# A convolution and attention kernel: first pixels ahead of the Toeplitz build, last sums ahead of last stores, two loads on another queue

## The chip, the cores and the metric

The kernel runs on one core of a Trainium2 chip. The metric is the device time of one execution, in microseconds, given as the median of several runs. A profile is one execution in which every instruction of every engine was recorded. The engines are TensorE (PE, with its weight loads as PEld), VectorE (DVE), ScalarE (ACT), GpSimd (POOL) and SyncE (SP). SP, ACT and POOL each also issue DMAs from a queue of their own, in order, mixed with their other instructions.

## The reference

Input x has 64 images of 55 x 55 pixels and 96 channels. Two layers follow each other; cut to what matters:

```python
# layer 0: depthwise 25x25 convolution of which only every third tap is kept
lat = conv(x, raw_kernel * mask)          # 9 x 9 taps, 3 pixels apart, the middle one left out
t = lat * x + bias + x                    # = (lat + 1) * x + bias
# layer 1: each image is a sequence of 3025 tokens
h = relu(bn1(layernorm(t) @ w1.T))        # 192 wide
X = fft(h, axis=tokens); ... diagonal complex map, relu ...; y = ifft(...).real
t = t + bn2(y @ w2.T)
t = t + ffn(layernorm(t))                 # 96 -> 384 -> 96, values rounded to fp8 and fp16
```

The change touches layer 0 and the place where layer 1 takes its sequences over.

## The kernel before

**Toeplitz build.** Taps that lie 3 pixels apart split the image into 3 residue classes of rows (r) and of columns. For each channel the 9 x 9 taps become a block matrix, so that the convolution of some rows is a few matrix products. PE makes these matrices from the taps (kt) and a 0/1 selector (sel, four loads): 56 slabs pt of 4 or 5 columns, each 8 or 10 matmuls into one of 8 PSUM banks (L205). ACT copies channels 0 to 47 of a slab into toep (L214), then DVE copies channels 48 to 95 into later (L215). later is written out to DRAM as tb in six stores on SP (L217), and toep is loaded anew from tb halfway through the convolution. Then the pools of this stage are closed with first.close(), and the buffers of the sums take their room: the first sum in such a buffer waits until everything that used the closed pools is done, the stores of tb among it.

**Convolution.** Work is cut into 12 groups (half of the channels, residue r, half of the images bh). A group has 4 tiles of rows for r = 0 and 3 tiles for r = 1 and 2, and 6 steps of 8 channels. A step loads its tiles' pixels x on SP (L234, 384 KB a tile, two buffers each, two steps ahead; the first two steps are asked for just before the loop). compute() multiplies: per tile and 4 channels, 16 matmuls for an outer tile and 24 for an inner one, into one PSUM bank pl (L253). DVE forms (pl + 1) * x in a buffer buf of the tile (L261, 0.84 us), and POOL adds the bias (L271). A tile has one buf through the six steps, and there are six bufs (NOB).

**Stores.** When a group ends, its bufs go to the DRAM tensor t1 in token order. stores() lists the DMAs of a tile: one large one a row on ACT (288 KB), and three small ones for three rows on POOL; in the last group every second large one is on SP. Most wait in pending and are issued a few at a time during the next group (L326). If the two groups together need more than six bufs, the first tiles' stores are issued at once, right after their last sums (early, L315). In the last group early is 3, so each tile's stores stand ahead of the next tile's sums.

**The order** in the convolution is written out by hand: each queue holds its instructions as the loop issues them. DMAs of SP and ACT take one of eight semaphores in turn, and each waits until that semaphore's last DMA has landed; POOL's DMAs have eight of their own.

**Sequences.** Layer 1 runs as 64 sequences whose tasks are ordered ahead of time by a planner (ordered(), with a cost and a due time for each task). sequence() begins with load(), two DMAs on SP of 112 and 9 rows (L527), into one of five t buffers. DVE takes the statistics (L538), ACT and DVE a root and its inverse (L499, L503), POOL scales (L552), PE turns and multiplies (L565, L586, L601), and so on. Two tables, m1 and m2, are loaded on ACT as the sequences begin, after the last stores on that queue (L67).

Of the kernel before, what the change touches and what calls it, by code (L numbers as in the profile page):

```python
# [11 lines left out]
F32 = mybir.dt.float32  # L12
# [8 lines left out]
B, R, CH = 64, 55, 96  # L21
NTOK = R * R
# [19 lines left out]
NOB = 6  # L42
SU = 21

NR1, NJ = 25, 121
# [3 lines left out]


@with_exitstack
def conv_attn_hybrid(ctx, tc, a, out, t1, tb, gds, eds):
    nc = tc.nc

    def split(n):
# [18 lines left out]
    with ExitStack() as cx:  # L76
        ccst = cx.enter_context(tc.tile_pool(name="c_cst", bufs=1))
        toep = ccst.tile([128, CHH, NE * TQ], F32, tag="toep", name="toep")
        cbias = ccst.tile([128, CH], F32, tag="cbias", name="cbias")
        ps = cx.enter_context(tc.tile_pool(name="c_ps", bufs=8, space=PSUM))  # L80
        xp = cx.enter_context(tc.tile_pool(name="c_x", bufs=2))
# [1 line left out]
        selp = first.enter_context(tc.tile_pool(name="c_sel", bufs=1))  # L83
        pp = first.enter_context(tc.tile_pool(name="prep", bufs=1))
        lp = first.enter_context(tc.tile_pool(name="c_later", bufs=1))
        later = lp.tile([128, CHH, NE * TQ], F32, tag="later", name="later")
        kt = selp.tile([128, CH], F32, tag="kt", name="kt")
        nc.sync.dma_start(kt, a["taps"])
        sel = selp.tile([128, TQ, SU * TQ], F32, tag="sel", name="sel")
# [9 lines left out]
        for n, of in enumerate(vecs):  # L99
            n0, n1 = 4 * CH * n, min(4 * CH * (n + 1), 4 * (H + CH) + 2 * CH)  # L100
# [30 lines left out]
        nc.vector.memset(ones, 1.0 / CH)  # L131
        zero = pp.tile([3 * NR1, CH], F32, tag="zero", name="zero")
        nc.vector.memset(zero, 0.0)
        for of in (toep, later):
            nc.gpsimd.memset(of[:, :, : 2 * TQ], 0.0)
            nc.gpsimd.memset(of[:, :, 16 * TQ :], 0.0)
        make_identity(nc, ident)
# [19 lines left out]
        for k, width in ((1, H), (2, CH)):  # L157
            bn = bns[k]
            v, r, q = (pp.tile([128, width], F32, tag=f"{x}{k}", name=f"{x}{k}") for x in ("v", "sc", "sq"))
# [9 lines left out]
            row, of = (w1e[96:97, :], slice(96, 97)) if k == 1 else (bias2, slice(0, NR1))  # L169
# [28 lines left out]
        for j0 in range(0, TQ, 5):  # L198
            nj = min(5, TQ - j0)
            for e in range(2, 16):  # L200
                pt = ps.tile([128, 512], F32, tag="ps", name=f"pt_{e}_{j0}")
                for jj in range(nj):
                    for p in range(2):
                        u0 = (15 - e + 3 * p) * TQ
                        nc.tensor.matmul(  # L205
                            pt[64 * p : 64 * p + 64, jj * CH : (jj + 1) * CH],
                            sel[:, j0 + jj, u0 : u0 + 64],
                            kt,
                            start=True,
                            stop=True,  # L210
                        )
                src = pt[:, : nj * CH].rearrange("p (n c) -> p c n", n=nj)
                cols = slice(e * TQ + j0, e * TQ + j0 + nj)
                nc.scalar.copy(toep[:, :, cols], src[:, :CHH])  # L214
                nc.vector.tensor_copy(later[:, :, cols], src[:, CHH:])  # L215
        for c0 in range(0, CHH, CC):
            nc.sync.dma_start(tb[:, c0 : c0 + CC], later[:, c0 : c0 + CC])  # L217
        first.close()

        ob = cx.enter_context(tc.tile_pool(name="c_ob", bufs=NOB))
        groups = [(0, r, bh) for r, bh in ((0, 0), (1, 0), (0, 1), (1, 1), (2, 0), (2, 1))]
        halfway = groups[-1]
        groups += [(1, r, bh) for bh in range(BH) for r in range(NR)]
        steps = [(n, c0) for n in range(len(groups)) for c0 in range(0, CHH, CC)]
        xts, bufs_ = {}, {}

        def load(n, c0):
            half, r, bh = groups[n]  # L230
            c1 = half * CHH + c0
            for m in range(NTS[r]):
                x = xp.tile([128, CC, NBS], F32, tag=f"x{m}", name=f"x{m}_{n}_{c0}")
                nc.sync.dma_start(x, a["xc"][bh, sum(NTS[:r]) + m][:, c1 : c1 + CC, :])  # L234
                xts[n, c0, m] = x

        def compute(n, c0, m):
            half, r, bh = groups[n]
# [36 lines left out]
        def stores(n, m):  # L275

            half, r, bh = groups[n]
            rows_, buf, b0 = TPS[r], bufs_.pop((n, m)), bh * BB
            last = n == len(groups) - 1
            nr = len([i for i in range(rows_) if 3 * (rows_ * m + i) + r < R])  # L280
            large, small_ = [], []
            for i in range(nr):
                n0 = (3 * (rows_ * m + i) + r) * R
                large.append((
                    nc.sync if last and i % 2 else nc.scalar,
                    t1[b0 : b0 + BB, half, n0 : n0 + 48, :].rearrange("b (q s) c -> q b (s c)", s=3),
                    buf[at_row(i) : at_row(i) + 16].rearrange("q (b s) c -> q b (s c)", s=3),
                ))


            to = t1[b0 : b0 + BB, half].rearrange("b (y z) c -> y b (z c)", z=R)
# [12 lines left out]
        for step in steps[:2]:  # L304
            load(*step)
        for k, (n, c0) in enumerate(steps):
            nt = NTS[groups[n][1]]
            nxt = NTS[groups[n + 1][1]] if n + 1 < len(groups) else NOB
            ending = c0 + CC == CHH
            early = nt + nxt - NOB if ending else 0  # L310
            for m in range(nt):
                compute(n, c0, m)
                if m < early:
                    for queue, to, of in stores(n, m):
                        queue.dma_start(to, of)  # L315
# [202 lines left out]
    def sequence(b):  # L518
# [3 lines left out]

        def load():
            tt = make(t, "t", [NJ, 2, NR1, CHH])
            tv = t1[b].rearrange("h (j r) c -> j h r c", r=NR1)
            for p0, p1 in split(NJ):
                nc.sync.dma_start(tt[p0:p1], tv[p0:p1])  # L527

# [16 lines left out]
        for i in range(7):  # L545
# [281 lines left out]
        for q in range(5):  # L827
# [23 lines left out]
            k = task("PE", 0.82, at, inverse_k2, [fetched], new=[(py, "psn")], use=[e2])  # L851
            k = task("DVE", 0.65, at, residual, [k], use=[py, t])
# [6 lines left out]
        for i in range(7):  # L859
            g0, ng = 4 * i, min(4, NR1 - 4 * i)  # L860
            xc, xq, pq = ("xc", b, i), ("xq", b, i), ("pq", b, i)
# [31 lines left out]
            k = task("POOL", 0.03 + 0.19 * ng, at - 0.08, centre, [rstd], new=[(xc, "xc")], use=[t, mean])  # L893
            k = task("POOL", 0.03 + 0.18 * ng, at - 0.08, quantise, [k], new=[(xq, "xq")], use=[xc, ("rstdc", b)])
            k = kt = task("PE", 0.054 * ng, at, turn, [k] + ([kt] if i else []), new=[(pq, "psn")] + ([(tq, "tq")] if i == 0 else []), use=[xq])
            turned_.append(task("ACT", 0.1 + 0.087 * ng, at, turned, [k], use=[pq, tq]))
        hq_done = {}
        for s, k in np.ndindex(3, 3):
            n0, n1 = UPT * s, (UPT * (s + 1) if s < 2 else NJ * NR1)
            n = n1 - n0  # L900
# [35 lines left out]
            x = task("PE", 0.45, at, up, turned_[: (3, 5, 7)[s]], new=[(pu, "psw"), (y16, "y16")], use=[tq])  # L936
            x = task("DVE", 1.23, at, cast, [x], use=[pu, y16])
# [177 lines left out]
```

## Time and profile before

| | us |
|---|---|
| median of three runs | 4841.59 (4833.22 to 4843.41) |
| the profiled execution: time | 4838.86 |
| its span, first to last instruction | 4836.9 |
| PE busy | 4443.6 (92%) |
| DVE, ACT, POOL busy | 3228.9, 3015.1, 3055.8 |
| first matmul of the build, of the convolution, of the sequences | 15.83, 86.10, 1016.73 |
| last matmul of the convolution ends | 944.5 |

How to read it: busy times are sums over the whole span, and hide stages with different limits. The page also divides the span into 40 equal slices of 121 us, each digit the busy share in tenths. The chain of waits follows the work that ended last backwards, from each piece to what released it. A timeline row names an engine, a line, an operation, what it writes and reads, how many, and in brackets how long the engine sat idle before it and what ended that. An entry such as "SPq" is a queue issuing DMAs, not moving data.

### The profile page before, as it was taken

The numbers are of one execution on the slowest core, as the hardware profiler recorded it, in microseconds if no ns is written. First come the engines' busy times: TensorE is split into PE (matmuls) and PEld (weight loads), VectorE is DVE, ScalarE is ACT, GpSimd is POOL, SyncE is SP. The second block draws the span as 40 slices with busy tenths as digits, with TensorE's granted clock in tenths as the row PEclk, the third lists the DMA queues.
The fourth block names the chain that finished last, engine by engine and source line by source line (L and its number), as shares of the span: only waits on it lengthen the run. The fifth ranks groups of instructions, "written<-read, shape, count | busy, mean of one in ns | idle before, by whom it ended". The sixth has DMA issues, their size and how long they took to land.

```text
span 4836.9 us, 194306 instructions
## 1 busy us (share of the span) xinstructions
PE 4443.6 (92%) x83314; PEld 3541.4 (73%) x83314; DVE 3228.9 (67%) x7232; ACT 3015.1 (62%) x5947; POOL 3055.8 (63%) x4209
## 2 busy tenths in 40 slices
PE   7998898759999999999999999999999999999996
PEld 6998898747777777777777777777777777777774
DVE  4444353425777777777777777777777777777766
ACT  1000000047888787777887788888778778877774
POOL 1666575725666666666666666666666666666664
PEclk8999999979999999999999999999999999999996
DMA  4688887876666666666666666666666666666652
GB/s 162 166 197 226 223 203 193 192 173 150 170 171 168 165 173 167 162 169 163 166 171 170 166 173 172 168 167 170 169 167 162 168 164 166 168 169 173 169 150 65
DMA packets 572794, 823.10 MB, mean 170 GB/s; under 512 B 62127, under 2 KB 470276, under 8 KB 570268
## 3 DMA queue, kind: packets, MB, share of 16 engines
q1 hardware_dynamic: 442704, 736.10, 56.0%
q10 hardware_dynamic: 113036, 64.71, 7.0%
q0 software_dynamic: 16192, 9.86, 1.1%
q8 instruction: 654, 10.72, 0.9%
q14 instruction: 208, 1.70, 0.1%
HBM read 419.45 MB, written 390.64 MB: 167 GB/s over the span
## 4 chain that ended last, share of the span: by engine, by line
PE 43%; DVE 16%; POOL 12%; DMA 10%; ACT 10%; issue 7%; ACTq 2%; SPq 0%; POOLq 0%; DVEq 0%
PE pl L253 13%; PE pd L741 6%; PE ph L586 4%; PE pf L601 4%; DVE y L916 4%; POOL ot L971 4%; DMA gd<-g 3%; PE px L667 3%; DVE stc L848 3%; PE pd L751 3%; ACT hq L931 3%; DVE m L693 3%; DMA x<-in_xc_dram 2%; PE pq L884 2%; DVE t L842 2%
## 5 line engine op out<-in xcount | busy, mean ns | idle before, releaser
L693 DVE SCALAR_TENSOR_TENSOR m<-px,par,m 128x400 f32<-128x400 f32 x768 | 478.7, 623 | 703.7 <-ACT m L684 416.3
L253 PE MATMUL pl<-x,toep 128*64 128x96 f32 (+1 forms) x18432 | 791.7, 250 | 91.0 <-DVE buf L261 39.3
L253 PEld LDWEIGHTS pl<-x,toep 128*64 128x64 f32 (+1 forms) x18432 | 786.3, 137 | 96.4 <-issue 46.8
L916 DVE CAST y<-pu 128x1008 f16<-128x1008 f32 (+1 forms) x576 | 690.3, 1198 | 182.0 <-PE pu L907 182.0
L261 DVE SCALAR_TENSOR_TENSOR buf<-pl,x 121x384 f32<-121x384 f32 (+1 forms) x480 | 390.5, 843 | 492.3 <-PE pl L253 310.8
L931 ACT ACTIVATE hq<-z 128x1008 fp8e5<-128x1008 f16 (+1 forms) x576 | 606.2, 1052 | 135.6 <-DVE z L919 130.2
L586 PE MATMUL ph<-w1e,tnt 97*121 97x192 f32 x3200 | 674.6, 335 | 3.0 <-ACT e L780 0.8
L601 PE MATMUL pf<-h,f 121*128 121x384 f32 (+1 forms) x1664 | 667.1, 501 | 2.1 <-ACT h L595 1.9
L271 POOL TENSOR_TENSOR buf<-buf,cbias 121x768 f32<-121x768 f32 (+1 forms) x240 | 433.6, 1820 | 355.8 <-DVE buf L261 336.3
L586 PEld LDWEIGHTS ph<-w1e,tnt 97*121 97x121 f32 x3200 | 531.6, 185 | 141.7 <-DVE t L842 15.9
L499 ACT ACTIVATE sm_s_a<-sm_v_a,eps 121x25 f32<-121x25 f32 x64 | 20.3, 317 | 950.1 <-POOL sm_v_a L490 950.1
L595 ACT ACTIVATE h<-ph 121x384 f32<-121x384 f32 (+1 forms) x832 | 402.7, 485 | 177.8 <-PE ph L586 177.5
L667 PEld LDWEIGHTS px<-m,gt 50*64 50x64 f32 x24576 | 398.6, 135 | 126.3 <-issue 81.0
L667 PE MATMUL px<-m,gt 50*64 50x50 f32 x24576 | 447.8, 221 | 16.8 <-issue 7.7
L971 POOL TENSOR_TENSOR ot<-t,o 121x480 f32<-121x480 f32 x320 | 361.1, 1128 | 117.1 <-DVE o L965 117.1
L741 PEld LDWEIGHTS pd<-w2e,sm 128*64 128x64 f32 x8192 | 351.8, 138 | 113.5 <-issue 58.6
L605 ACT COPY g<-pf 128x384 f32<-128x384 f32 (+1 forms) x832 | 393.5, 473 | 61.7 <-PE pf L601 45.8
L700 POOL TENSOR_TENSOR sr<-ar,m 128x400 f32<-128x400 f32 x128 | 132.7, 1036 | 444.1 <-DVE m L693 434.1
L741 PE MATMUL pd<-w2e,sm 128*64 128x96 f32 x8192 | 410.0, 251 | 0.4 <-ACT h L595 0.4
L565 PE MATMUL pa<-ident,xa 121*96 121x121 f32 x1600 | 241.5, 268 | 162.3 <-POOL xa L552 72.2
L552 POOL TENSOR_TENSOR xa<-t,rstda 121x384 f32<-121x384 f32 (+1 forms) x448 | 346.9, 780 | 60.4 <-PE pa L565 55.4
L951 PEld LDWEIGHTS <-hq 128*121 128x121 fp8e5 x4800 | 331.5, 142 | 54.5 <-issue 21.7
(115 smaller groups left out, 8597.2 us busy)
## 6 DMA issues: line engine op xcount, KB each, us to landing
gd<-g SPq DMA_DIRECT2D x768, 192.0 KB
gt<-gd SPq DMA_DIRECT2D x512, 288.0 KB
x<-in_xc_dram SPq DMA_DIRECT2D x240, 384.0 KB
t<-t SPq DMA_DIRECT2D x64, 1050.0 KB
out_dram<-ot SPq DMA_DIRECT2D x320, 210.0 KB
t<-buf ACTq DMA_DIRECT2D x211, 288.0 KB
ed<-e SPq DMA_DIRECT2D x384, 150.0 KB
ed<-e SPq DMA_DIRECT2D x128, 131.2 KB
```

The lines of the kernel that those rows point to most:

```text
L253: nc.tensor.matmul(pl[p : p + width, cc * NBS : (cc + 1) * NBS], toep[:, c0 + g + cc, o : o + width], xts[n, c0, m + d][:, g + cc, :], sta ...
L271: nc.gpsimd.tensor_tensor(part, part, cbias[:px, c1 : c1 + CC].unsqueeze(1).to_broadcast([px, NBS, CC]), ALU.add)
L586: nc.tensor.matmul(x[:NJ, q * H : (q + 1) * H], live[tnt][:, g * NJ : (g + 1) * NJ], w1e, start=True, stop=True,)
L595: nc.scalar.activation(live[h][:, : nq * H], live[ph][:NJ, : nq * H], AF.Relu)
L601: nc.tensor.matmul(x[:, : nq * H], f1, live[h][:, : nq * H], start=True, stop=True)
L605: nc.scalar.copy(live[g][:, q0 : q0 + nq].rearrange("p q c -> p (q c)"), live[pf][:, : nq * H])
L667: nc.tensor.matmul(x[to : to + 64].rearrange("p (q r n) -> p q r n", q=2, r=2)[:, k2p, :, o : o + NR1], y[rows, k % KC, c0 : c0 + 64], m1[ ...
L693: nc.vector.scalar_tensor_tensor(live[out_], view(px)[:, :, 256 : 256 + KC * NR1], scale, live[than], ALU.mult, ALU.max)
L741: nc.tensor.matmul(y[k % 2][64 * k2p : 64 * k2p + 64, k // 2 * CH : (k // 2 + 1) * CH], full[:, k, 64 * k2p : 64 * k2p + 64], w2e[:, 0, :] ...
L916: nc.vector.tensor_copy(live[y16][:, :n], live[pu][:, :n])
L931: nc.scalar.activation(live[hq][:, k, n0 : n0 + n], live[z16][:, :n], AF.Copy, saturate=False)
L971: nc.gpsimd.tensor_tensor(halves(y), live[t][:, :, 5 * q : 5 * q + 5], halves(live[o16]), ALU.add)
```

## The change

Six things are changed. The first two steps' pixels are asked for at the very top, ahead of taps and selectors. The group list, which now stands there too, begins with r = 1 for each half of the images where it began with r = 0. later is three tiles of 16 channels; each slab's copy by DVE is three copies, and each of the six stores reads one of the tiles. In the last group no tile's stores are issued inside the loop over tiles; all come after the last sum. t1 is two tensors, one for each half of the images. Sequences 0 and 1 are loaded by one DMA each on GpSimd's queue; the other 62 as before.

```diff
-        later = lp.tile([128, CHH, NE * TQ], F32, tag="later", name="later")
+        later = [lp.tile([128, CPL, NE * TQ], F32, tag=f"later{k}", name=f"later{k}") for k in range(CHH // CPL)]
+        groups = [(0, r, bh) for r, bh in ((1, 0), (0, 0), (1, 1), (0, 1), (2, 0), (2, 1))]
+        halfway = groups[-1]
+        groups += [(1, r, bh) for bh in range(BH) for r in range(NR)]
+        steps = [(n, c0) for n in range(len(groups)) for c0 in range(0, CHH, CC)]
...
+        for step in steps[:2]:
+            load(*step)
         kt = selp.tile([128, CH], F32, tag="kt", name="kt")
         nc.sync.dma_start(kt, a["taps"])
...
-        for of in (toep, later):
+        for of in (toep, *later):
             nc.gpsimd.memset(of[:, :, : 2 * TQ], 0.0)
             nc.gpsimd.memset(of[:, :, 16 * TQ :], 0.0)
...
                 nc.scalar.copy(toep[:, :, cols], src[:, :CHH])
-                nc.vector.tensor_copy(later[:, :, cols], src[:, CHH:])
+                for k, of in enumerate(later):
+                    c1 = CHH + CPL * k
+                    nc.vector.tensor_copy(of[:, :, cols], src[:, c1 : c1 + CPL])
         for c0 in range(0, CHH, CC):
-            nc.sync.dma_start(tb[:, c0 : c0 + CC], later[:, c0 : c0 + CC])
+            k, c1 = c0 // CPL, c0 % CPL
+            nc.sync.dma_start(tb[:, c0 : c0 + CC], later[k][:, c1 : c1 + CC])
         first.close()
...
-        groups = [(0, r, bh) for r, bh in ((0, 0), (1, 0), (0, 1), (1, 1), (2, 0), (2, 1))]
...
-        for step in steps[:2]:
-            load(*step)
...
-                if m < early:
+                if m < early and n + 1 < len(groups):
                     for queue, to, of in stores(n, m):
                         queue.dma_start(to, of)
...
-                pending = [x for m in range(max(0, early), nt) for x in stores(n, m)]
+                pending = [x for m in range(nt) if (n, m) in bufs_ for x in stores(n, m)]
...
-            tv = t1[b].rearrange("h (j r) c -> j h r c", r=NR1)
+            tv = t1s[b // BB][b % BB].rearrange("h (j r) c -> j h r c", r=NR1)
+            if b < 2:
+
+                nc.gpsimd.dma_start(tt, tv)
+                return
             for p0, p1 in split(NJ):
                 nc.sync.dma_start(tt[p0:p1], tv[p0:p1])
...
-            t1 = dp.tile([B, 2, NTOK, CHH], F32, tag="t1", name="t1")
+            t1s = [dp.tile([BB, 2, NTOK, CHH], F32, tag=f"t1_{k}", name=f"t1_{k}") for k in range(BH)]
```

More of the change, by code (lines that the diff above doesn't have):

```diff
@@ L42 @@
 NOB = 6
+CPL = 16
 SU = 21
@@ L53, in conv_attn_hybrid @@
 @with_exitstack
-def conv_attn_hybrid(ctx, tc, a, out, t1, tb, gds, eds):
+def conv_attn_hybrid(ctx, tc, a, out, t1s, tb, gds, eds):
     nc = tc.nc
@@ L85, in conv_attn_hybrid, with load @@
         lp = first.enter_context(tc.tile_pool(name="c_later", bufs=1))
-        later = lp.tile([128, CHH, NE * TQ], F32, tag="later", name="later")
+        later = [lp.tile([128, CPL, NE * TQ], F32, tag=f"later{k}", name=f"later{k}") for k in range(CHH // CPL)]
[3 more added lines that the diff above has]
+        steps = [(n, c0) for n in range(len(groups)) for c0 in range(0, CHH, CC)]
+        xts, bufs_ = {}, {}
+        def load(n, c0):
+            half, r, bh = groups[n]
+            c1 = half * CHH + c0
+            for m in range(NTS[r]):
+                x = xp.tile([128, CC, NBS], F32, tag=f"x{m}", name=f"x{m}_{n}_{c0}")
+                nc.sync.dma_start(x, a["xc"][bh, sum(NTS[:r]) + m][:, c1 : c1 + CC, :])
+                xts[n, c0, m] = x
+        for step in steps[:2]:
+            load(*step)
         kt = selp.tile([128, CH], F32, tag="kt", name="kt")
@@ L214, in conv_attn_hybrid @@
                 nc.scalar.copy(toep[:, :, cols], src[:, :CHH])
-                nc.vector.tensor_copy(later[:, :, cols], src[:, CHH:])
+                for k, of in enumerate(later):
+                    c1 = CHH + CPL * k
+                    nc.vector.tensor_copy(of[:, :, cols], src[:, c1 : c1 + CPL])
         for c0 in range(0, CHH, CC):
-            nc.sync.dma_start(tb[:, c0 : c0 + CC], later[:, c0 : c0 + CC])
+            k, c1 = c0 // CPL, c0 % CPL
+            nc.sync.dma_start(tb[:, c0 : c0 + CC], later[k][:, c1 : c1 + CC])
         first.close()
         ob = cx.enter_context(tc.tile_pool(name="c_ob", bufs=NOB))
-        groups = [(0, r, bh) for r, bh in ((0, 0), (1, 0), (0, 1), (1, 1), (2, 0), (2, 1))]
[L224 to L235, printed above, removed]
         def compute(n, c0, m):
@@ L277, in stores @@
             half, r, bh = groups[n]
-            rows_, buf, b0 = TPS[r], bufs_.pop((n, m)), bh * BB
+            rows_, buf = TPS[r], bufs_.pop((n, m))
             last = n == len(groups) - 1
@@ L285, in stores @@
                     nc.sync if last and i % 2 else nc.scalar,
-                    t1[b0 : b0 + BB, half, n0 : n0 + 48, :].rearrange("b (q s) c -> q b (s c)", s=3),
+                    t1s[bh][:, half, n0 : n0 + 48, :].rearrange("b (q s) c -> q b (s c)", s=3),
                     buf[at_row(i) : at_row(i) + 16].rearrange("q (b s) c -> q b (s c)", s=3),
                 ))
-            to = t1[b0 : b0 + BB, half].rearrange("b (y z) c -> y b (z c)", z=R)
+            to = t1s[bh][:, half].rearrange("b (y z) c -> y b (z c)", z=R)
             for i0, (q, ns) in itertools.product(range(0, nr, 3), ((16, 3), (17, 3), (18, 1))):
@@ L1111 @@
             eds = [dp.tile([NR1, 4, KHP, CH], F32, tag=f"e{k}", name=f"ed{k}") for k in range(2)]
-            conv_attn_hybrid(tc, a, out, t1, tb, gds, eds)
+            conv_attn_hybrid(tc, a, out, t1s, tb, gds, eds)
     r = run(nc, [arrays], core_ids=[0])
```

## The prediction

> **What bounds the kernel now.** I read the page's busy slices first, then three stretches: the start, the convolution, and the hand-over to the sequences. The slices show TensorE (PE) nearly full except at two dents, slice 8 and, less deep, the first slices:
>
> ```profile
> PE   7998898759999999999999999999999999999996
> ...
> DMA  4688887876666666666666666666666666666652
> ```
>
> From slice 9 on PE is at 9 tenths to the last slice, and the diff adds or removes nothing there, so those 3,800 us only shift. The change lives in the first 1,020 us. The windows view (columns: stretch, its length, busy time and count of PE, PE loads, VectorE = DVE, ScalarE = ACT, GpSimd = POOL, granted clock, DMA share, GB/s) and the chain of waits for the start:
>
> ```profile
> 40.00:60.00 20.00, 20.00 (x491) 20.00 (x489) 10.42 (x27) 9.87 (x27) 0.00 (x0) 1.00 0.01 4
> 60.00:80.00 20.00, 1.81 (x44) 1.62 (x40) 1.45 (x4) 1.28 (x4) 0.00 (x0) 0.60 0.84 350
> ...
> 100.00:120.00 20.00, 20.00 (x491) 20.00 (x489) 10.83 (x13) 0.00 (x0) 11.57 (x7) 1.00 0.45 140
> ```
>
> ```profile
> 15.83 46.01 PE pt L205 x1064
> ...
> 69.63 17.45 DMA x<-in_xc_dram
> 87.08 0.14 issue
> 87.22 82.94 PE pl L253 x1954
> ```
>
> PE builds the Toeplitz tiles to 61.8, then sits idle for 25 us until 87.2, because the first pixels stand on SyncE's queue (SP) behind the six stores of the second half; meanwhile during the build the DMA engines moved 4 GB/s. A finer windows view dates those stores: 438 GB/s up to 82, a dip in the next line, where the pixels take over, so they are in by about 83.5.
>
> ```profile
> 80.00:82.00 2.00, 0.00 (x0) 0.00 (x0) 0.00 (x0) 0.00 (x0) 0.00 (x0) 0.50 1.04 438
> 82.00:84.00 2.00, 0.00 (x0) 0.00 (x0) 0.00 (x0) 0.00 (x0) 0.00 (x0) 0.50 1.01 263
> ```
>
> The convolution (87 to 944.5) has 18,432 matmul records. One PE timeline row has 734 of them in 30.44 us, 41.5 ns each, so 764 us at full clock; 93 us of the stage is loss. The PE timeline's gaps sum to some 66 us, mostly DVE waiting for a buffer whose store had not landed; the worst is the first line here. The rest is the halved clock after gaps. The hand-over is the second line:
>
> ```profile
> 462.92 5.12 PE L253 MATMUL pl<-x,toep 128*64 128x96 f32 x72 [11.15 <-DVE buf L261]
> ```
>
> ```profile
> 1016.73 1.85 PE L565 MATMUL pa<-ident,xa 121*96 121x121 f32 x8 [72.21 <-POOL xa L552]
> ```
>
> ```profile
> 944.07 1.81 POOL L271 TENSOR_TENSOR buf<-buf,cbias 121x768 f32<-121x768 f32 x1
> ...
> 956.20 1.80 POOL L271 TENSOR_TENSOR buf<-buf,cbias 121x768 f32<-121x768 f32 x1
> 958.30 3.95 POOL L315 DMA_DIRECT2D t<-buf  x6 [0.31 <-POOL buf L271]
> ```
>
> ```profile
> 985.37 23.89 SPq L527 DMA_DIRECT2D t<-t  x10
> ```
>
> ```profile
> 1012.62 1.69 DVE L538 BATCH_NORM_STATS2 sta<-t 121x6 f32<-121x96 f32 x10 [2.82 <-DMA t<-t]
> 1014.23 0.29 DVE L503 RECIPROCAL rstda<-sm_s_a 121x25 f32<-121x25 f32 x1
> 1014.44 2.42 DVE L538 BATCH_NORM_STATS2 sta<-t 121x6 f32<-121x96 f32 x15
> 1017.98 2.49 DVE L538 BATCH_NORM_STATS2 sta<-t 121x6 f32<-121x96 f32 x15 [1.12 <-DMA t<-t]
> ```
>
> The last sum waits until 956.2 behind small stores on POOL, the ten loads start at 985.4 behind SP's nine last stores, and DVE's order makes sequence 0's root wait for sequence 1's load (1012.6) and sequence 1's for sequence 2's (1018.0).
>
> **What the Trainium skill says.** "DMA: Bandwidth & Descriptors", section "Queues, rings and completion order": each DMA engine takes turns between the queues packet by packet. The page of before agrees that packets differ: ACT's queue moved 64.71 MB in 113,036 packets, 572 bytes each, while a row of a sequence's load is 4,800 bytes, so a load beside the stores gets more than its turn. The same page, "Why a DMA increments its semaphore by 16 and not by 1": the number of engines is the largest divisor up to 16 of the slow dimension, 11 for 121 rows, with an exception for GpSimd's queue that uses all; no run shows which. "TensorE: Matmul & The Clock Gate", Part 1: an idle window halves the clock until PE is busy again. The trace agrees: half clock from about 64 to 91.5, so 2 us are lost after 87.2.
>
> **The change part by part.** Queue orders are those of the built program.
>
> *Pixels first.* Six x loads (384 KB each) go ahead of the taps and the four selector loads on SP, so past those, eight pads of ed and the six stores. DMAs of SP and ACT share eight semaphores in turn and each waits for its semaphore's last user, so the first selector load now waits for fw1's landing, fw1's issue for the second x, and taps for the fourth x. 2.36 MB at the 425 GB/s of the 60 to 80 stretch is 5.5 us. But PE's first build matmul was held by pm (14.88), behind ACT's table load at 8.76, not by the selectors; I estimate both at about 16.5 to 17.5. Cost 1.7 us, between 0.5 and, were all queueing exposed, 5.5.
>
> *Three tiles.* 56 copies by DVE become 168. Back to back the old ones start 0.31 us apart (20.57, 20.88, 21.20) for 240 elements; a third each is between 0.10 and 0.31, and I take 0.15, so 0.45 per slab of 0.82 us of PE (46.01/56). Hidden by PE; at 0.31 a slab takes 0.93 and costs 6 us. The last slab adds 0.1. Six memsets in place of two move the same elements on idle POOL. The split doesn't free anything early: in the new program DVE's first sum still waits for all six stores.
>
> *Start of the convolution.* PE may start at about 64 with x there, and fills eight PSUM banks: with the three-tile group first that is 2(16+24+16)+2x16 = 144 matmuls of two records, 144 x 83 ns = 11.9 us. Then it waits for DVE, which waits for the stores: 83.5 + 1.8 = 85.3, one sum of 0.84, so 86.2. Lead against 87.2: 11.9 + 1.0 = **12.9 us**; the half clock is met in both. The next x loads are issued as DVE frees tiles (from 87 on), with 6.6 us of matmuls in hand; covered. Bounds 8 and 14.
>
> *Group order.* With three tiles first, stores begin after 55 us of matmuls instead of 79, and with the lead about 38 us earlier, into a stretch where DMA is at 0.34 to 0.45. Nt runs 3,4,3,4,3,3 instead of 4,3,4,3,3,3, so only two lean groups follow each other before the reload of toep. About 50 of the 93 us of loss lie there (446 to 557). Bounds: nothing, and 25; a loss of 16 if a boundary turns worse (below). I take **8 us**.
>
> *Last sums, two loads on GpSimd.* The three last sums end near 947 instead of 958; 12 small stores move behind them. 18 small stores follow, 0.66 us to issue each, eight semaphores, some 10 us to land: about 22 us, then five memsets (1.3 us), then the loads of sequences 0 and 1 at about 970. They no longer wait behind SP (985.4). SP loses four issues (2.33, 3.01, 1.08, 1.12). Beside the stores they should land near 980 and 988; queued behind them on POOL are only sums that need them. Next late is sequence 2's load on SP, which shares the engines with m1 and m2 (1.87 MB, ACT). DMA was at 0.75 to 0.82 from 944 to 972: moving 2.3 MB there uses about 5 us that were idle, the displaced stores end later by the rest; m1 and m2 no longer take turns with the first loads (3 to 4 us), and the earlier last stores give a few. Sequence 2 in at about 1006 instead of 1018: **12 us**. Bounds 4 (t0 and t1 on few engines, landing after it) and 20.
>
> Sum: 12.9 + 8 + 12 = 33. Profiled execution 4838.9 (span 4836.9 and 2 around it) less 33 is **4806**; the median of 4841.6 is 2.7 above that execution, so 0.7% below.
>
> **Rivals.** (B) One gain is hidden: DMA bounds the convolution (0.8 and more after 180), so its end doesn't move though its start does, or the last stores drain no earlier and sequence 2 lands as before. 0.8 shares that never reach 1 speak for it; PE at 99% in 300 to 400 against. 13 to 20 us left: 4822. (C) The stalls of 446 to 557 vanish and the tail gives 20: 12.9 + 22 + 20, 4784; for it the 40 us of stores moved into idle time, against it the reload that stays. (N) Both of B, with only the head's lead partly kept: 4835. (S) Slower: the place is the boundary between groups. Two neighbouring groups with seven tiles share six buffers, so one tile's stores must land within some 16 us; among the first five boundaries the new order has four such in place of three, and DVE waits there. Price 11.15 plus 5 of half clock, 16 each. It decides from the third stall on, when it eats the 33: with a loss of 16, 4855. Against it: the added boundary comes when no other stores are queued.
>
> **How the numbers follow.** Forecast 0.46 (own range 4796 to 4819), B 0.24, C 0.14, N 0.09, S 0.07. About 0.2% (9.7 us) can be told from no change. B, C and the forecast are faster: 0.84; N same: 0.09; S slower: 0.07. The range reaches to 4781 for C and 4829 for B.
>
> **What would show it.** PE's first pl near 64, a gap from 76 to 86, then full. First ACT stores near 125 instead of 160.8. The end of matmuls near 924. POOL's last sums in a row, its t loads about 25 us after them, PE's pa some 60 us after the last pl instead of 72. Wrong if PE's first pl waits for x, if pt begins after 20, if gaps with DVE buf grow, or if the pace after the hand-over changes from about 60 us a sequence ((4836.9 - 1016.7)/64).

## The result, and the profile after

| | before | after |
|---|---|---|
| median of 20 runs each, us | 4839.79 (4827.8 to 4853.4) | 4816.01 (4798.85 to 4834.27) |
| profiled execution: time; span | 4838.86; 4836.9 | 4798.85; 4797.1 |
| build by PE ends | 61.8 | 60.5 |
| convolution: first matmul; last one ends | 86.1; 944.5 | 60.3; 918.7 |
| first matmul of the sequences | 1016.7 | 971.8 |
| from the convolution's last matmul to the end of the span | 3892.4 | 3878.3 |

The ratio of the times is 0.9948, with a 95% interval of 0.9936 to 0.996: 25 us less, between 19 and 31. The profiled execution of after is the shortest of its 20, so the two profiles stand 40 us apart where the medians stand 24; below, dates from single profiles are used for order and for waits, and amounts are means over several profiles or come from the ratios.

The busy slices of after (tenths in 40 slices of 120 us) answer to the first view of before:

```profile
PE   8999898689999999999999999999999999999996
...
DMA  4788888875666666666666666666666666666662
```

The first three digits of PE were 7, 9 and 9 and are 8, 9 and 9. The dent at the hand-over, a 5 in the ninth digit of before (slice 8, counted from 0), is a 6 in the eighth: it comes earlier. From the tenth digit on the row of nines is the same, only shorter. At the start, PE's timeline of after has (start, length, engine, line, operation, count; in brackets the idle time before and what ended it):

```profile
59.80 0.66 PE L225 MATMUL pt<-kt,sel 128*64 128x96 f32 x12
60.30 11.39 PE L261 MATMUL pl<-x,toep 128*64 128x96 f32 x272
72.52 0.88 PE L261 MATMUL pl<-x,toep 128*64 128x96 f32 x16 [0.83 <-issue]
85.62 14.58 PE L261 MATMUL pl<-x,toep 128*64 128x96 f32 x306 [12.22 <-DVE buf L269]
```

The first pl follows the last pt without a gap, so the pixels were there. PE does 272 + 16 records, which are 144 matmuls of two records each, and then stands for 12.2 us. DVE's timeline and the chain of waits (start, length, what) of after name the cause:

```profile
84.76 5.51 DVE L269 SCALAR_TENSOR_TENSOR buf<-pl,x 121x384 f32<-121x384 f32 x8 [23.39 <-DMA tb<-later]
```

```profile
66.78 17.57 DMA tb<-later
84.76 0.81 DVE buf L269
```

DVE may not write the first sum before the six stores of tb have landed. The idle time has moved from before the first matmul to after the 144th; what was won is the work done ahead of it. The windows view (columns as in the prediction) shows the stores of t coming forward:

```profile
60.00:80.00 20.00, 12.56 (x300) 12.18 (x296) 1.02 (x7) 0.55 (x2) 0.00 (x0) 0.89 0.92 379
120.00:140.00 20.00, 19.97 (x484) 19.86 (x482) 10.24 (x13) 0.00 (x0) 16.31 (x13) 1.00 0.76 186
```

From 120 to 140 DMA is at 0.76 where it was at 0.34; ACT's first store is issued at 127.35 where it was 160.76. At the other end, the timelines of PE, POOL, SP's queue and DVE in after, in this order:

```profile
971.81 1.85 PE L575 MATMUL pa<-ident,xa 121*96 121x121 f32 x8 [53.07 <-POOL xa L562]
```

```profile
915.01 1.81 POOL L279 TENSOR_TENSOR buf<-buf,cbias 121x768 f32<-121x768 f32 x1 [1.08 <-DVE buf L269]
...
919.66 1.78 POOL L279 TENSOR_TENSOR buf<-buf,cbias 121x768 f32<-121x768 f32 x1 [2.83 <-DVE buf L269]
921.38 5.26 POOL L335 DMA_DIRECT2D t<-buf  x8
...
943.53 1.60 POOL L534 DMA_DIRECT2D t<-t  x2
```

```profile
962.77 11.83 SPq L537 DMA_DIRECT2D t<-t  x6
```

```profile
961.62 4.09 DVE L548 BATCH_NORM_STATS2 sta<-t 121x6 f32<-121x96 f32 x25 [42.05 <-DMA t<-t]
966.50 1.70 DVE L548 BATCH_NORM_STATS2 sta<-t 121x6 f32<-121x96 f32 x10 [0.79 <-DMA t<-t]
969.29 0.32 DVE L509 RECIPROCAL rstda<-sm_s_a 121x25 f32<-121x25 f32 x1 [1.09 <-ACT sm_s_a L505]
...
980.08 2.49 DVE L548 BATCH_NORM_STATS2 sta<-t 121x6 f32<-121x96 f32 x15 [8.13 <-DMA t<-t]
982.49 0.30 DVE L509 RECIPROCAL rstda<-sm_s_a 121x25 f32<-121x25 f32 x1
```

POOL's last sum follows DVE's last sum at once, the small stores come after it, and the two loads are issued at 943.5, 19 us before SP issues the next. PE starts on the sequences 53 us after its last matmul of the convolution, where it was 72. But sequence 1's root (982.49) stands on DVE behind statistics of sequence 2, whose load on SP lands only at 980. What that load waits for is in the view of SP's waits from 913 to 980 (engine, line, what for; us in total, times, longest):

```profile
SPq L537 <- DMA t<-buf: 20.6, 3, 10.8
```

Before the first of the load's two DMAs (issued at 962.77) SP waits 10.8 us for a store of its own to land, and before the second, the one of 9 rows (972.67), another 9.6 us for a store of ACT, with which it shares one of the eight semaphores.

### The profile page after: what moved, and what is told of

Read it like the earlier page. It is cut to its first block, busy times and chain, and to the rows that moved or that the text cites. A ratio compares the mean times of both kernels' runs of the same rounds, so it can differ in the third digit from the quotient of the medians.

```text
span 4797.1 us, 194464 instructions
## 1 busy us (share of the span) xinstructions
PE 4431.4 (92%) x83314; PEld 3528.9 (74%) x83314; DVE 3233.7 (67%) x7344; ACT 3011.1 (63%) x5947; POOL 3057.1 (64%) x4215
## 4 chain that ended last, share of the span: by engine, by line
PE 39%; DVE 20%; POOL 13%; DMA 10%; ACT 8%; issue 8%; ACTq 1%; SPq 0%; POOLq 0%; DVEq 0%
PE pl L261 12%; PE pd L751 5%; DVE y L926 4%; DVE stc L858 4%; PE pf L611 4%; PE ph L596 4%; POOL ot L981 4%; DMA gd<-g 3%; PE pd L761 3%; DVE m L703 3%; ACT hq L941 3%; DVE t L852 3%; PE px L677 2%; DMA gt<-gd 2%; DMA t<-buf 2%
## 5 line engine op out<-in xcount | busy, mean ns | idle before, releaser
L261 PE MATMUL pl<-x,toep 128*64 128x96 f32 (+1 forms) x18432 | 784.9, 249 | 73.6 <-DVE buf L269 43.4
L694 ACT ACTIVATE m<-px,par 128x400 f32<-128x400 f32 x384 | 262.6, 684 | 170.8 <-PE px L677 166.3
```

The lines of the kernel that those rows point to most:

```text
L261: nc.tensor.matmul(pl[p : p + width, cc * NBS : (cc + 1) * NBS], toep[:, c0 + g + cc, o : o + width], xts[n, c0, m + d][:, g + cc, :], sta ...
```

## The experiments

None of the twelve leaves out a part of the computation. "Last matmul" is the end of the convolution's last matmul; "2nd root" (the reciprocal of sequence 1 on DVE) and "end" are counted from it. All four dates are from one profiled execution each. "mid" is the sum of PE's gaps over 0.3 us between 430 and 580, around the reload of toep. Each ratio is to runs of before that were taken beside that kernel's, so it isn't the ratio of two medians of this document.

| run | median, us (runs) | ratio, 95% | last matmul | mid | 2nd root | end |
|---|---|---|---|---|---|---|
| before | | | 944.5 | 33.2 | 77.6 | 3892.4 |
| after | 4816.0 (20) | 0.9948 (0.9936, 0.996) | 918.7 | 26.4 | 63.8 | 3878.3 |
| e1_head_only | 4818.4 (9) | 0.9953 (0.9934, 0.9972) | 916.2 | 23.6 | 76.0 | 3886.5 |
| e2_tail_only | 4830.0 (14) | 0.9991 (0.9977, 1.0006) | 946.8 | 31.3 | 63.4 | 3890.2 |
| e3_old_group_order | 4813.0 (8) | 0.9945 (0.9926, 0.9965) | 936.8 | 30.9 | 63.0 | 3880.6 |
| e4_one_later_tile | 4812.6 (12) | 0.9949 (0.9934, 0.9964) | 930.5 | 26.5 | 67.4 | 3880.3 |
| e5_loads_on_sync | 4819.7 (14) | 0.9954 (0.9942, 0.9966) | 937.5 | 24.5 | 68.9 | 3889.1 |
| e6_stores_between_sums | 4819.2 (5) | 0.9961 (0.9948, 0.9974) | 919.5 | 23.6 | 74.2 | 3897.8 |
| e7_three_on_gpsimd | 4810.9 (6) | 0.9938 (0.9915, 0.9962) | 926.2 | 21.4 | 69.0 | 3891.1 |
| e8_five_on_gpsimd | 4812.3 (6) | 0.995 (0.9935, 0.9965) | 928.1 | 24.4 | 68.9 | 3879.0 |
| e9_order_only | 4835.9 (14) | 0.9995 (0.998, 1.0009) | 929.2 | 22.8 | 75.5 | 3893.0 |
| e10_pixels_only | 4833.1 (21) | 0.9982 (0.9971, 0.9993) | 932.6 | 32.1 | 72.3 | 3887.0 |
| e11_two_free_buffers | 4818.2 (5) | 0.9962 (0.9949, 0.9975) | 931.5 | 29.3 | 64.0 | 3877.6 |
| a2_changed_again | 4809.4 (5) | 0.9941 (0.9928, 0.9954) | 929.0 | 23.1 | 64.0 | 3879.2 |

**The head without the tail, and the tail without the head.** e1 is the changed kernel with the last group's stores and all loads as before:

```diff
-                if m < early and n + 1 < len(groups):
+                if m < early:
...
-            if b < 2:
-
-                nc.gpsimd.dma_start(tt, tv)
-                return
```

> The changed kernel with its tail undone: last stores between the sums and sequences 0 and 1 loaded on SyncE as before; pixels first, three tiles and the new group order kept. If the parts simply add (theory A), the convolution ends near 919 to 924 in its profile, the sequences' first turn comes some 72 us after that as before, and the time is 14 to 26 us under the kernel before. If the convolution is bound by its stores so that the lead is eaten (rival B), its end moves by less than 8 us and the time by less than that.

e2 is the kernel before with those two edits the other way round, and pending filled as in the changed kernel:

```diff
-                if m < early:
+                if m < early and n + 1 < len(groups):
...
+            if b < 2:
+
+                nc.gpsimd.dma_start(tt, tv)
+                return
```

> The kernel before with the tail alone: all sums of the last group ahead of its stores, sequences 0 and 1 loaded on GpSimd. Theory A: convolution ends near 944, first turn of a sequence some 53 us later, second batch of scaling near 1008 in place of 1024.8, time 10 to 18 us under before. Rival B, that all of the median gain is the tail: 20 to 26 us under before. If the tail only reorders loads that share the DMA engines (rival C), second batch within 4 us of before and no change of the time.

Measured: the head alone takes off 23 us by its ratio (14 to 32), the tail alone 4 (11 less to 3 more). So most of the gain is the head's. In e2's profile the convolution ends at 946.8, as before, the second root comes 63.4 after it instead of 77.6, and yet the end comes only 2.2 us earlier (3890.2 against 3892.4). The tail moves the loads as it should, but in this one profile most of what it wins is lost again before the end; 10 to 18 us were expected of the time, and that is not seen. The means over more profiles, further down, are kinder to the tail. The split of t1 in two tensors has no run of its own: e2 does without it and issues its two loads 26.8 us after the last matmul, after 24.8.

**The group order taken back, and alone.** e3 is the changed kernel, e9 the kernel before, each with the other's list:

```diff
-        groups = [(0, r, bh) for r, bh in ((1, 0), (0, 0), (1, 1), (0, 1), (2, 0), (2, 1))]
+        groups = [(0, r, bh) for r, bh in ((0, 0), (1, 0), (0, 1), (1, 1), (2, 0), (2, 1))]
```

(e3; e9 is the reverse.)

> The changed kernel with the old order of groups (four-tile group first); all else kept. If the order gives about half of the head's gain, as the prediction's 8 us, the convolution ends 8 to 13 us later than in the changed kernel and the time is 8 to 13 us above it. If the order does nothing, within 3 us of it. If starting the stores earlier hurts, faster than the changed kernel.

> The kernel before with the new group order alone, pixels still behind the six stores. By the prediction's term (8 us, from stores that begin after 55 instead of 79 us of matmuls) 5 to 10 us under before, and the gaps of the convolution smaller by as much. If the order does nothing, as the old order inside the changed kernel suggested (4813 against 4816), within 4 us of before. If it needs the lead to pay, also within 4 us.

Measured: neither time tells the order from nothing. e3 at 0.9945 lies inside the interval of the changed kernel, e9 at 0.9995 takes off 2.4 us (10 less to 4 more). The gaps tell more. PE's timeline of e3, then of e9, at the boundary ahead of the reload of toep; before, this wait was 11.15 us:

```profile
455.96 12.26 PE L261 MATMUL pl<-x,toep 128*64 128x96 f32 x224 [12.64 <-DVE buf L269]
```

```profile
454.32 5.45 PE L253 MATMUL pl<-x,toep 128*64 128x96 f32 x72 [5.07 <-DVE buf L261]
```

Every profile with the old order has one wait of 10.2 to 12.6 us here (with the new order the longest of the whole stage past 100 us is 5.7 to 7.5), and a sum "mid" of 30.9 to 33.2 (before, e2, e3, e10; mean 31.9). With the new order and six equal buffers the sum is 21.4 to 26.5 in all nine profiles (mean 24.0). The two sets don't overlap: the order saves 7.9 us of waits in this stretch. Over the whole convolution past 100 us such gaps sum to 67.0 with the old order and 59.2 with the new on the same means, though there the sets do overlap. Whether it is the earlier stores or the spacing of the lean groups that saves them is not told apart. The order doesn't take all waits away; these two from PE's timeline of after stay:

```profile
516.65 5.46 PE L261 MATMUL pl<-x,toep 128*64 128x96 f32 x96 [7.11 <-DVE buf L269]
528.61 62.87 PE L261 MATMUL pl<-x,toep 128*64 128x96 f32 x1467 [6.50 <-DVE buf L269]
```

Why e3's median isn't some 8 us above the changed kernel's stays open; its interval reaches to 0.9965, which leaves room for it.

**One later tile.** e4 is the changed kernel with later in one piece:

```diff
-                for k, of in enumerate(later):
-                    c1 = CHH + CPL * k
-                    nc.vector.tensor_copy(of[:, :, cols], src[:, c1 : c1 + CPL])
+                nc.vector.tensor_copy(later[:, :, cols], src[:, CHH:])
```

> The changed kernel with the second half in one tile again, 56 copies by DVE in place of 168. Theory: the copies lie beside PE's build and the first sum waits for all six stores either way, so the build ends within 0.3 us of the changed kernel, PE's second wait ends at the same time within 1 us, and the time is within 3 us. Rival, that three tiles let buffers be taken earlier: the gap before 85.6 grows by several us.

Measured: 0.9949 against the changed kernel's 0.9948. The three tiles neither cost nor bring anything that shows. DVE's copies stand beside PE, and DVE's last ones in after end less than a microsecond behind PE's last pt:

```profile
60.26 1.11 DVE L237 COPY later<-pt 128x64 f32<-128x64 f32 x6 [0.21 <-ACT toep L234]
```

Six in 1.11 us are 0.185 us each, 0.55 for three, against 0.82 us of PE for a slab.

**The pixels alone.** e10 is the changed kernel with the old order, one later tile and the old tail, so that of the edits that move work only this is left:

```diff
+        for step in steps[:2]:
+            load(*step)
         kt = selp.tile([128, CH], F32, tag="kt", name="kt")
...
         pending = []
-        for step in steps[:2]:
-            load(*step)
```

> The kernel before with one thing changed: the first two steps' pixels are asked for ahead of taps and selectors; old group order, one later tile, old tail. Theory A': the pixels alone are most of the head's gain; with a four-tile group first PE fills eight banks with 2(16+24+24+16) = 160 matmuls, 13.3 us, before it waits for the six stores, so the lead at PE's restart is 13 to 15 us, and the time is 12 to 20 us under the kernel before. Rival: half of the head's gain needs the new group order; then 6 to 10 us under before.

PE's timeline of e10:

```profile
63.92 12.46 PE L258 MATMUL pl<-x,toep 128*64 128x96 f32 x297
77.15 1.20 PE L258 MATMUL pl<-x,toep 128*64 128x96 f32 x23 [0.77 <-issue]
89.25 10.94 PE L258 MATMUL pl<-x,toep 128*64 128x96 f32 x198 [10.90 <-DVE buf L266]
```

With a group of four tiles first, eight PSUM banks hold 320 records, 160 matmuls: 13.2 us of work. It goes on at 89.25 where before went on at 87.2, since the build ended 2.3 us later, so the lead is 11.2 us. By the ratio it takes off 8.7 us (3 to 14). That is under the 12 to 20 that were expected of it, and inside the 6 to 10 of the rival, that half of the head's gain needs the new order. The mechanism at the start is as thought; how much of the lead is kept to the end isn't known better than this.

**One half of the tail at a time.** e5 is the changed kernel without the loads on GpSimd (last sums first), e6 the changed kernel with the stores between the sums again (loads on GpSimd):

```diff
-            if b < 2:
-
-                nc.gpsimd.dma_start(tt, tv)
-                return
```

(e5)

> The changed kernel with sequences 0 and 1 loaded on SyncE as before, last sums still ahead of last stores. If the gain of the tail is that two loads no longer wait behind SyncE's nine stores, the second root (the second reciprocal on DVE) comes 72 to 77 us after the last convolution matmul in place of 64, and the time is 4 to 10 us above the changed kernel. If the tail's gain is the sums' place, it keeps the 64 and the time.

```diff
-                if m < early and n + 1 < len(groups):
+                if m < early:
```

(e6)

> The changed kernel with the last group's stores between its sums again, the two loads still on GpSimd. If the sums' place gave part of the gain, the last sum ends some 10 us later and the first two loads, behind fewer small stores but the same number in all, are issued within 3 us of the changed kernel's 25 us after the last matmul; time 2 to 5 us above it. If only the loads' queue matters, time within 3 us.

Measured: end is 3889.1 and 3897.8, no better than the old tail's 3886.5 to 3893.0, and the ratios are 0.9954 and 0.9961. Neither half is seen to bring anything alone, but these are single ends, and the intervals of the ratios overlap the changed kernel's. DVE's timeline of e5, then of e6:

```profile
984.61 4.09 DVE L544 BATCH_NORM_STATS2 sta<-t 121x6 f32<-121x96 f32 x25 [46.28 <-DMA t<-t]
996.91 1.69 DVE L544 BATCH_NORM_STATS2 sta<-t 121x6 f32<-121x96 f32 x10 [8.21 <-DMA t<-t]
```

```profile
974.22 0.32 DVE L509 RECIPROCAL rstda<-sm_s_a 121x25 f32<-121x25 f32 x1 [6.95 <-ACT sm_s_a L505]
...
991.31 2.49 DVE L548 BATCH_NORM_STATS2 sta<-t 121x6 f32<-121x96 f32 x15 [14.43 <-DMA t<-t]
```

In e5 sequence 1 is late (8.21 us of waiting): before the second of its two DMAs SP stood 11.0 us until a store of ACT on the same semaphore had landed. The second root comes at 68.9, between the 72 to 77 and the 64 that were expected. In e6 sequences 0 and 1 are there at 961 and 966, 41 and 46 us after the last matmul (43 and 48 in after). Then DVE waits 6.95 us for ACT, which issues its last stores, m1 and m2 until 973.8 and only then comes to the first root. Last, sequence 2 holds the second root for 14.43 us. Both DMAs of its load are issued at 52 us after the last matmul in e6, at 44.0 and 53.9 in after; yet it is used only 20 us after the second in e6, and 7.4 in after. What makes that difference was not taken apart.

**More loads on GpSimd.** e7 and e8 put three and five loads there:

```diff
-            if b < 2:
+            if b < 3:
```

(e7; b < 5 in e8.)

> The changed kernel with sequences 0, 1 and 2 loaded on GpSimd. In the changed kernel DVE waited 8.1 us for sequence 2's load, which SyncE issued at 962.8, 19 us after the two of GpSimd. If that load's place on the queue gates the second root, it comes 5 to 9 us earlier (55 to 59 us after the last convolution matmul) and the time falls by 3 to 8 us. If the DMA engines' total work gates it, the second root moves less than 3 us and the time stays within 3 us.

> The changed kernel with the first five sequences loaded on GpSimd. If the queue gates the loads, as many as possible before SyncE's last store: time 2 to 8 us under the changed kernel. If the engines' total work gates, the five compete with the last stores and with m1 and m2, and the time is within 3 us of it or above.

Measured: 0.9938 and 0.995, both with the changed kernel's 0.9948 in their intervals. DVE's timeline of e7:

```profile
977.66 1.70 DVE L548 BATCH_NORM_STATS2 sta<-t 121x6 f32<-121x96 f32 x10 [4.42 <-DMA t<-t]
984.53 0.32 DVE L509 RECIPROCAL rstda<-sm_s_a 121x25 f32<-121x25 f32 x1 [5.18 <-ACT sm_s_a L505]
984.76 4.82 DVE L548 BATCH_NORM_STATS2 sta<-t 121x6 f32<-121x96 f32 x30
```

The wait for sequence 2 is gone (30 statistics in a row), and still the second root comes at 69.0 in e7 and 68.9 in e8, where it comes at 63.0 to 67.4 in the five profiles with this tail and two loads. In e7 no load holds it any more; ACT does. ACT's timeline of e7 (ACT counts as idle while its queue issues DMAs, hence the 921.05):

```profile
936.74 42.78 ACTq L335 DMA_DIRECT2D t<-buf  x9
979.63 4.50 ACTq L68 DMA_DIRECT2D m<-in_m_dram  x2
984.18 0.32 ACT L505 ACTIVATE sm_s_a<-sm_v_a,eps 121x25 f32<-121x25 f32 x1 [921.05 <-DMA t<-buf]
...
994.17 0.87 ACT L605 ACTIVATE h<-ph 121x384 f32<-121x384 f32 x2 [4.66 <-DMA t<-buf]
```

The first root's input is ready at 974.7, but ACT is issuing its nine last stores, m1 and m2, and comes to the root at 984.18. The second root stands behind the first h on ACT, which waits 4.66 us for one of the stores to land. In e8 it stands behind the same h, which waits 8.83 us for a DMA, by the trace a load. In after the first root is held so for only 1.8 us. So with three loads taken from SP the next in-order queue, ACT's, sets the date. That is read from the traces; no run takes ACT's stores or tables away.

The end of e7, 3891.1 in a profiled execution 8 us above the run's median, suggests that a single profile's end can be off by some 10 us. "DMA: Bandwidth & Descriptors" in the Trainium skill, section "Issuing engines are not separate DMA queues", says that DMAs of all engines end on the same 16 DMA engines, so that another queue saves only time of issuing. The times fit that, since a third and a fifth load bring nothing measurable; but these two runs don't test it, since ACT stands between the loads and the root.

**Two buffers that don't wait for the stores.** e11 (e7 with two more pools) tries to win the 12.2 us gap. Two of the six buffers lie where the selectors lay, and only the other four wait for later's stores:

```diff
+        oba = cx.enter_context(tc.tile_pool(name="c_oba", bufs=2))
+        early_bufs = [oba.tile([128, NBS, CHH], F32, tag="buf", name=f"buf_e{i}") for i in range(2)]
+        second.close()
+        obb = cx.enter_context(tc.tile_pool(name="c_obb", bufs=NOB - 2, side="right"))
```

> The changed kernel with sequence 2 on GpSimd too, and the room of the sums' buffers split: two of the six lie where selectors and parameters were, which nobody reads after the build, so only the other four wait for the six stores. If that wait is what ends PE's first run at 144 matmuls, PE now goes on until the third tile's sums are due: four banks come free early, 144 + 80 = 224 matmuls before the wait, the 12 us gap falls to 5 to 6 us, and the time is 4 to 7 us under the kernel with three sequences on GpSimd. Rival, that the convolution's stores bound it later: the gap shrinks and the time doesn't move.

> The changed kernel itself once more, for the spread of its stages from one execution to another. If the 40 us between the two profiled executions are typical, its convolution ends near 919 again. If that execution was at the lucky end, as its own 4799 against a median of 4816 says, the convolution ends at 925 to 937 and the time from the last convolution matmul to the end is 3878 to 3890.

a2 is the changed kernel itself, run beside it. PE's timeline of e11:

```profile
61.37 11.40 PE L269 MATMUL pl<-x,toep 128*64 128x96 f32 x272
73.57 5.50 PE L269 MATMUL pl<-x,toep 128*64 128x96 f32 x128 [0.80 <-issue]
81.14 2.19 PE L269 MATMUL pl<-x,toep 128*64 128x96 f32 x48 [2.07 <-issue]
86.92 0.38 PE L269 MATMUL pl<-x,toep 128*64 128x96 f32 x4 [3.59 <-DMA x<-in_xc_dram]
```

PE now does 448 records, 224 matmuls, before 84, where the changed kernel does 144: 6.6 us more work done. Then the next pixels are late, since they stand on SP behind the six stores. Nothing of it reached the end: 4818.2 against 4809.4 for a2 and 4810.9 for e7, where 4 to 7 us under e7 were expected. Past 100 us PE's gaps over 0.3 us sum to 71.6 us in e11 and to 62.1 in a2 (51.7 to 67.8 in the nine profiles with six equal buffers and the new order). So the 6.6 us of work won at the start are met by some 9 us more of waits. By the view of PE's waits from 100 to 945, 3.6 us more of them are for pixels (16.4 against 12.8) and 5.3 more are gaps that end with nothing the profile shows (27.1 against 21.8); those for DVE's buffers are the same (28.9 and 28.5). Whether DMA's share or the fixed turn of two unequal pools makes them wasn't taken apart. None of these versions is shown to be faster than the changed kernel.

## Why the prediction was right, and where a term was off

The forecast was 33 us less and 4806; the runs give 25 less (19 to 31) and 4816. The time lies in the forecast's own range (4796 to 4819), though its size is nearer to rival B's 4822 than to 4806; what speaks against B is where the time came from. The direction and the three places were right; one term of the sum, the last, was too large.

- **Pixels first, 12.9.** As written: x there at the end of the build, 144 matmuls in eight banks, a gap of 12.2 us that ends with the stores of tb, and PE back at 85.6 (86.2 forecast). The lead in after is 11.9 + 87.2 - 85.6 = 13.5 us, in e10 11.2. Of the cost put on the start of the build, 1.7 us, little shows: the build's first matmul is at 15.3 in after and between there and 17.6 in the runs with this edit, and between 15.6 and 16.9 in those without.
- **Three tiles, 0.** Right (e4). A copy takes 0.185 us where 0.15 was taken, and stays hidden.
- **Group order, 8.** The stretch was the right one, and the amount too in waits: 31.9 us of gaps become 24.0. That it was 22 (rival C) is excluded by the two waits that stay. The times are too scattered to show it by themselves.
- **Both together.** The eight profiles with this head and the plain six buffers (after, e1, e4 to e8, a2) end the convolution at 925.7 on the mean, before and e2 at 945.7: 20 us, where 12.9 + 8 = 20.9 were forecast. So close an agreement is partly luck: the profiled executions of before and e2 lie 4 us above the medians of their runs on the mean, the eight 2 below. Against rival B, in which the lead of the start is lost to the DMAs of the convolution, stands e1's time too, 23 us less (14 to 32) with the old tail. In e11 the added lead was lost; whether to DMA isn't shown.
- **The last sums and two loads, 12.** This is the term that was mis-sized. Its dates came out in the pair of profiles: the loads were issued 25 us after the last matmul (24.8), sequence 2 was in 61.3 us after it (61.5 forecast); PE's first pa came after 53 us, not some 60. t0 and t1 landed 18 and 22 us after their issue, not 10 and 18, so what the prediction gave them over the stores for their larger packets was too much; no run shows that the packets which the profile counts are those between which it has the DMA engines take turns. The date of sequence 2 owes something to luck. The prediction had it set by what its load shares the engines with; the traces of the five profiles with this tail (after, e2, e3, e4, a2) show a wait that it left out here. The second DMA of that load waits 3.4 to 24.2 us for a store of ACT on the same semaphore, and goes out 53.3 to 56.3 us after the last matmul, whether the first went out at 31.8 or at 50.4; DVE has the sequence 7 to 8.4 us later. No run removes that wait by itself.
- **The step in it that failed** is the one from "sequence 2 in 12 us earlier" to "the end 12 us earlier". The second root comes 64.3 us after the last matmul with this tail (mean of after, e2, e3, e4, a2) and 75.3 without it (before, e1, e9, e10): 11 us. The end comes after 3881.7 and 3889.7: **8 us**. The times alone would give less: 4.4 in e2, 2.4 between e1 and after, each uncertain by more than that.

Where do those 3 us go? The first matmul px of the sequences, which comes behind work on sequence 1, starts 96.9 after the last matmul with the new tail and 104.6 without it on the same means: 7.6 earlier. So they are gone between the second root and px. The timelines of POOL, ACT and PE in after:

```profile
982.86 0.23 POOL L513 TENSOR_TENSOR sm_s_a<-rstda 121x25 f32<-121x25 f32 x1 [6.93 <-DVE rstda L509]
```

```profile
986.15 0.32 ACT L505 ACTIVATE sm_s_a<-sm_v_a,eps 121x25 f32<-121x25 f32 x1 [3.65 <-POOL sm_v_a L496]
```

```profile
987.25 1.65 PE L611 MATMUL pf<-h,f 121*128 121x384 f32 x2 [3.56 <-ACT h L605]
```

POOL stands 6.93 us for sequence 1's root. What follows it on POOL comes late, so the root of sequence 2 on ACT does too, and behind that root stands h. PE, 19 us ahead of before at its first pa, then idles for h. From the second root to px such waits are its only ones over 0.15 us in all nine profiles. They sum to 0.33 us in each of the four without the tail, and 3.56, 4.92, 3.24, 0.33 and 4.70 in the five with it, 3.0 more on the mean. So PE, started early on the first sequence, waits for the later ones, and that is where the 3 us went.

From px to the end nothing more is lost on these means (7.6 and 8 us), and the pace doesn't change, as forecast: from the second root to the end are 3814.8 us before and 3814.6 after. The three parts measured alone by their ratios (8.7, 2.4 and 4.4 us) sum to 15.5, the whole is 25; with intervals of 5 to 7 us each way this is no proof that they help each other, and it stays open.

Rival S, longer stalls at the group boundaries, was wrong: the longest wait at a boundary fell from 11.15 to 7.11 us. One sign of being wrong that the prediction named, growing gaps with DVE buf, appears if taken by the letter: on the pages they are 39.3 us before and 43.4 after. But 12.2 of these are the gap at 85.6, which was itself forecast; past it they fall to 31.1.

## What to carry to other kernels

Work brought forward across a wait is worth what can be done before the next wait on the same resource: count the buffers (here eight PSUM banks, 144 matmuls) and price only that. At a hand-over, follow the last load that the in-order engines need, not the first, and look at what it waits for: here a semaphore shared with another queue's stores. When that load is out of the way, ask which in-order queue comes next; here it was ACT's, and moving a third and a fifth load brought nothing that could be measured. Compare sums of gaps in the stretch where an edit should act before trusting medians that scatter by more than the edit.

## What the runs showed of the hardware

Two profiled executions of the same program (after and a2) differ by 11 us in span (4797.1 and 4808.1), and 10.2 of these lie before the convolution's last matmul, which ends at 918.7 and 929.0; from there to the end they agree within 1 us (3878.3 and 3879.2). In this pair the scatter is made before the hand-over, not in the 3,800 us after it. That isn't so of every run: from the last matmul to the end the five profiles with this tail lie between 3878.3 and 3890.2.

During the last stores, DMA was busy 0.83 of the time from 918 to 944 and moved 160 GB/s, as this windows line of after shows, while the stores of tb moved 438 GB/s at the start:

```profile
918.00:944.00 26.00, 0.74 (x17) 0.54 (x13) 0.80 (x1) 0.00 (x0) 15.16 (x25) 0.58 0.83 160
```

So a share of 0.8 need not mean a rate near the highest that was seen. And a queue's time for its DMAs is not all issuing: SP's nine last stores in after stand in its timeline for 37.6 us, of which some 19 are the nine issues themselves (0.3 to 5.1 us each) and the rest waits for an earlier store to land. Of the 23.9 us of the ten loads of before, 13.7 are waits for a DMA to land, 12.8 of them for m1 and m2.
